# Two layers of cross attention and experts: Silu written through tanh, and part of the convolution and of the last residuals moved from VectorE to ScalarE and GpSimd

## The chip, the cores and the metric

The kernel runs on one core of a Trainium2 chip. The metric is device time in microseconds (us), the median of several runs. The engines of the core are named as in the profile: PE (TensorE, matrix products) with PEld (its weight load), DVE (VectorE), ACT (ScalarE), POOL (GpSimd) and SP (SyncE, which issues transfers). Each engine works through its own queue of instructions in order and waits for the others by semaphores.

## The reference, cut to what matters

`x` has 2 sequences of 1024 tokens with 256 features. Two layers of attention and experts follow each other, each added to `x`:

```python
x = x + L0_xattn(ctx, layernorm(x))    # 16 heads of 64; 77 context rows ask, 1101 keys
x = x + L0_ffn(layernorm(x))           # 8 experts, the best 2 of each token, Relu inside;
                                       # its own last step is a layernorm with gamma, beta
x = x + L1_xattn(layernorm(x), ctx)    # 16 heads of 16, 77 keys, causal
x = x + L1_ffn(layernorm(x))

# L1_ffn, with h its input and cw the weights of the best 2 of 8 experts
g, u = h @ Wg[e], h @ Wu[e]                        # e = 0..3
routed = sum(cw[e] * ((silu(g) * u) @ Wd[e]))
routed += (cw[4] + cw[6]) * h + cw[7] * relu(h)    # experts without a matrix
shared = causal convolution of h over 4 tokens, feature by feature, + conv_b
return routed + shared
```

All is float32. The two places that the change touches are `silu(g) * u` and the convolution of the last step, and the layernorm that ends `L0_ffn` for tokens of the last quarter: `x + (a - mean) * rstd * gamma + beta`, where `a` is the layer's input plus what the experts gave.

## The kernel before, in words

The tokens lie in 16 tiles of 128 rows (`xr[:, t, :]`), four tiles to a block, so that the last quarter is block 3 with tiles 12 to 15. The first layer's attention takes the greater part of the run. Then come 39 slots, each one expert's work on 128 gathered tokens (`up`, `down`, lines 1230 to 1265). Beside the later slots, and after the last one, the second layer runs, block by block, in numbered steps `k`; this part begins around 1400 us, and the last slot ends near 1540 us.

The order of the instructions on every engine is written out by hand: `tc.manual_schedule` (line 1666) keeps all five queues in the order in which the program calls its functions. There is no planner that moves anything. Four tables say what is called in a step: `pre` and `mid` (attention: `project`, `turn_back`, `divide`, `attend`), `rest` (the second expert layer's `up` and `down`) and `fill` (all else). A step first does its attention part with `score`, `turn_step` and `soften` (softmax: maximum and subtraction on DVE, lines 1322 and 1323, Exp on ACT, line 1324), then `rest`, then `fill` (lines 1715 to 1721).

What the change touches:

- `Mix.up(e)` (line 1503) multiplies the block's 512 tokens by `Wg[e]` and `Wu[e]` (line 1510, tile `pg`), applies Silu on ACT (line 1518, tile `sl`, 128 x 512) and multiplies by the second product on DVE (line 1522, tile `hid`). `Mix.down(e)` multiplies `hid` by `Wd[e]` (line 1533) and adds the weighted result to `xr` on DVE (line 1541). There are 16 pairs, four to a block. Those of blocks 0 to 2 come in steps 18 to 43, beside attention; those of block 3 come last, in steps 45 to 52, with no attention left.
- `Mix.convolve(c)` (line 1481) is called twice a block, in the steps of `up(1)` and `up(2)`: the first term on ACT (line 1487) and three taps on DVE (line 1491), all of them into the one tile `cv`. `Mix.convolved` turns it back and adds it to `xr` (lines 1500 and 1501). `Mix.copies` (lines 1475 to 1479) treats the experts without a matrix, with two ACT operations and two POOL additions of 128 x 256 for each tile; it is called in steps next to those of `convolve`.
- `way(t, put)` (line 1585) lays out the path of tile `t` from the first expert layer to the second attention, in successive steps: `weigh` (line 1018) and `measure(0, t)`, then `residual(t)` (lines 1032 and 1033, two DVE operations) and `measure(1, t)` (statistics of the new `xr`, line 141 ff. on DVE, the power -0.5 on POOL, line 156), then `shift(1, t)` (line 1027) and `normal(t)` (line 1040 on ACT, line 1041 on POOL), then the transposes and the queries. For tiles 12 to 15 this goes in `fill`, a step apart, between steps 22 and 29; for the tiles before, it goes beside the slots. `gather(t)` (line 1001, two indirect transfers issued by POOL) precedes it.

POOL's queue in this part holds gathers, the powers of the statistics, line 1041 and the additions of `copies`.

Of the kernel before, what the change touches and what calls it, by code (L numbers as in the profile page):

```python
# [8 lines left out]
F32 = mybir.dt.float32  # L9
I32 = mybir.dt.int32  # L10
AF = mybir.ActivationFunctionType
ALU = mybir.AluOpType
# [4 lines left out]
P = 128  # L17
# [3 lines left out]
NBLK = 4  # L21
# [25 lines left out]
E1, EM, I1, KC = 8, 4, 128, 4  # L47
# [3 lines left out]
def tile_two_layers(ctx: ExitStack, tc: tile.TileContext, a: dict, out: bass.AP):  # L51
    nc = tc.nc
# [12 lines left out]
    xr = const.tile([P, NT, D], F32, tag="xr", name="xr")  # L65
# [423 lines left out]
    side = {}  # L489
# [75 lines left out]
    with ExitStack() as st:  # L565
# [5 lines left out]
        ps_s = st.enter_context(tc.tile_pool(name="a_ps_s", bufs=1, space=PSUM))  # L571
# [50 lines left out]
        def contexts():  # L622
            src = [ctx_sb[:, b, :] for b in range(B)]
            stats = ln_stats(src)
            ch = lnp.tile([C, B, D], F32, tag="ch", name="ch")
            yield
            ln_apply([ch[:, b, :] for b in range(B)], src, stats)
            for b in range(B):
                for c in range(2):
                    pt = ps_t.tile([P, 512], F32, tag="t", name="pt")  # L630
                    nc.tensor.transpose(pt[:, :C], ch[:, b, c * P : (c + 1) * P], ident[:C, :C])
                    nc.vector.tensor_scalar(
                        kvT[b][:, c, S:NKEY], pt[:, :C], ln1w[:, c : c + 1], ln1b[:, c : c + 1], ALU.mult, ALU.add
                    )
# [202 lines left out]
        with tc.manual_schedule(engines=ORDERED):  # L837
# [14 lines left out]
            c = contexts()  # L852
# [31 lines left out]
            for n in range(2):  # L884
                m, s, v, t = latents(2 + n)
# [102 lines left out]
    got, stat, qT_of, h_at, hT_at = {}, {}, {}, {}, {}  # L988
# [24 lines left out]
    def acc(t):  # L1013
        return tok[t // 8][:, t % 8, :]
# [15 lines left out]
    def residual(t):  # L1030
        mv, rstd = stat.pop((0, t))
        nc.vector.scalar_tensor_tensor(acc(t), acc(t), mv[:, 0, 0:1], gamma, ALU.subtract, ALU.mult)
        nc.vector.scalar_tensor_tensor(xr[:, t, :], acc(t), rstd[:, :1], xr[:, t, :], ALU.mult, ALU.add)


    def normal(t):

        nb, rstd = stat.pop((1, t))
        h = h_at[t] = en.tile([P, D], F32, tag="h", name="h")
        nc.scalar.activation(h, xr[:, t, :], AF.Identity, bias=nb[:, :1], scale=rstd[:, :1])  # L1040
        nc.gpsimd.tensor_tensor(xr[:, t, :], xr[:, t, :], bo1, ALU.add)
# [48 lines left out]
    en = ctx.enter_context(tc.tile_pool(name="en", bufs=2, side="right", reuse_waits="tile"))  # L1090
    ps_h = ctx.enter_context(tc.tile_pool(name="b_ps_h", bufs=2, space=PSUM, reuse_waits="tile"))
    ps_o = ctx.enter_context(tc.tile_pool(name="b_ps_o", bufs=1, space=PSUM, reuse_waits="tile"))
    extra, first, spare = ExitStack(), ExitStack(), ExitStack()

    ps_x = spare.enter_context(tc.tile_pool(name="b_ps_x", bufs=1, space=PSUM, reuse_waits="tile"))
    hp = ctx.enter_context(tc.tile_pool(name="b_h", bufs=2, side="right", reuse_waits="tile"))
    yp = ctx.enter_context(tc.tile_pool(name="b_y", bufs=2, side="right", reuse_waits="tile"))
    xp = ctx.enter_context(tc.tile_pool(name="b_x", bufs=3, side="right", reuse_waits="tile"))
    xe = first.enter_context(tc.tile_pool(name="b_xe", bufs=1, side="right", reuse_waits="tile"))

    fw = [
# [1 line left out]
        for i in range(4)  # L1103
    ]
    xs_of = {s: xe.tile([P, D], F32, tag=f"xs{s}", name="xs") for s in (*range(3, NA), 2, 0, 1)}
    at_p = ps_s = None
    later = {}

    def table():
# [65 lines left out]
    def ask_rows(s):  # L1175

        r0 = entry(nc.sync, s, 1)
        xs = xs_of[s] if s < NA else xp.tile([P, D], F32, tag="xs", name="xs")
        nc.sync.dma_start(out=xs, in_=tab_x[bass.ds(r0, TB), :])
        rows_of[s] = xs  # L1180
# [37 lines left out]
    def turn_rows(s):  # L1218
        xs = rows_of.pop(s)
        pt = ps_t.tile([P, 512], F32, tag="t", name="px")  # L1220
        for c in range(2):
            nc.tensor.transpose(pt[:, c * TB : (c + 1) * TB], xs[:, c * P : (c + 1) * P], ident)
        xT = xp.tile([P, 2, TB], F32, tag="xT", name="xT", bufs=2)
        evac(xT.rearrange("p c q -> p (c q)"), pt[:, : 2 * TB], to=nc.vector)
        return xT

    def hidden(s):
        return hp.tile([P, NF, TB], F32, tag="hT", name="hT")
# [163 lines left out]
    class Mix:  # L1392
# [88 lines left out]
        def convolve(self, c):  # L1481

            if c == 0:
                self.cv = at_p.tile([P, 2, 512], F32, tag="cv", name="cv", bufs=1)
            cv = self.cv[:, c, :]
            src = hT2[self.b][:, c, self.off - KC + 1 : self.off + 512]
            nc.scalar.activation(
                cv, src[:, :512], AF.Identity, bias=cb1[:, c : c + 1], scale=cw1[:, c * KC : c * KC + 1]
            )
            for k in range(1, KC):  # L1490
                nc.vector.scalar_tensor_tensor(
                    cv, src[:, k : k + 512], cw1[:, c * KC + k : c * KC + k + 1], cv, ALU.mult, ALU.add
                )
# [9 lines left out]
        def up(self, e):  # L1503
            ps = []
            for w in (wg1, wu1):
                ups[0] += 1
                pool = ps_x if ps_x is not None and ups[0] % 3 == 0 else ps_h
                ps.append(pool.tile([P, 512], F32, tag="h", name="pg"))
                for c in range(2):
                    nc.tensor.matmul(  # L1510
                        ps[-1],
                        w[:, e, c, :],
                        hT2[self.b][:, c, self.off : self.off + 512],
                        start=(c == 0),
                        stop=(c == 1),
                    )
            sl = rp.tile([P, 2, 512], F32, tag="tT", name="sl", bufs=1)[:, 0, :]
            nc.scalar.activation(sl, ps[0], AF.Silu)

            hid = const.tile([P, 2, D], F32, tag="l1w" + "kv"[e % 2], name="hid").rearrange("p c d -> p (c d)")  # L1520
            self.hid[e] = hid
            nc.vector.tensor_tensor(hid, sl, ps[1], ALU.mult)

        def down(self, e):
            hid = self.hid.pop(e)
# [59 lines left out]
    def way(t, put):  # L1585

        put(1, weigh, t)
        put(1, measure, 0, t)
        put(2, residual, t)
        put(2, measure, 1, t)  # L1590
        put(3, shift, 1, t)
        put(3, normal, t)
        put(4, turned, t)
        put(5, queries, t)
# [13 lines left out]
    def put(where, k, f, *args):  # L1608
        where.setdefault(k, []).append((f, args))
# [18 lines left out]
    for t in range(12, NT):  # L1628
        k = K1 + t - 12
# [7 lines left out]
    for n, (blk, e) in enumerate(halves):  # L1637
        m = mix[blk]
        k = at_step[2 * n : 2 * n + 2]
# [12 lines left out]
    def run_all(where, k):  # L1652
        for f, args in where.pop(k, []):
            f(*args)
# [11 lines left out]
    with tc.manual_schedule(engines=ORDERED | {mybir.EngineType.SP}):  # L1666
        ask_rows(0)
        ask(0)
        ask_rows(1)
        ask(1)  # L1670
        for s in range(2, NA):
            if s < 4:
                ask(s)
            ask_rows(s)
        xT = turn_rows(0)
        r3.measure()
        r3.stats()
        prev, k = None, 0
        for s in range(NSLOT):
            hT = hidden(s)  # L1680
            up(s, xT, hT, 0)
            for f in todo.pop(s, []):
                f()
            if s > S1:
                step(k)
                run_all(fill, k)
            up(s, xT, hT, 1)
            if s + 1 < NSLOT:
                xT = turn_rows(s + 1)
            if s == NA:  # L1690
                first.close()
            if prev is not None:
                down(*prev)
                ask_later(s)
            if s == S1:
                extra.close()
                spare.close()
                ps_x = None
                kbd, v1p, causal = spread["s"]
                at_p = ctx.enter_context(tc.tile_pool(name="c_at", bufs=1, reuse_waits="tile"))  # L1700
                ps_s = spare.enter_context(tc.tile_pool(name="c_ps_s", bufs=1, space=PSUM, reuse_waits="tile"))
                step(k)
                run_all(fill, k)
            if s >= S1:
                step(k + 1)
                run_all(rest, k)
                run_all(rest, k + 1)
                run_all(fill, k + 1)
                k += 2
            prev = s, hT  # L1710
            for f in todo.pop(s + 0.5, []):
                f()
        down(*prev)
        assert not todo and k == K1, todo
        for k in range(K1, K3 + 8):
            if k == K3:
                spare.close()
                ps_x = ctx.enter_context(tc.tile_pool(name="d_ps_x", bufs=1, space=PSUM, reuse_waits="tile"))
            step(k)
            run_all(rest, k)  # L1720
            run_all(fill, k)
        mix[-1].down(EM - 1)
        assert not fill and not pre and not mid and not rest, (fill, pre, mid, rest)
# [59 lines left out]
```

## Time and profile before

| | us |
|---|---|
| median of 3 runs | 1721.43 (1720.8 to 1727.57) |
| the profiled execution | 1722.1 |
| its span | 1720.4 |
| PE busy in the span | 1634.9 (95%) |
| DVE | 1077.2 (63%) |
| POOL | 850.1 (49%) |
| ACT | 732.7 (43%) |
| mean granted PE clock | 0.988 of full speed |

The shares are means over unlike stages: POOL's 850 us are nearly all from the first attention, and after 1530 us POOL is busy for some 44 of 190 us. A matrix product's end is modelled in the trace, so a busy PE need not be PE at its peak. In the chain of waits, each line is the piece of work, or the wait for none that the profile shows ("issue"), that the end of the run is followed back through.

### The profile page before, as it was taken

Reading aid. Unit: us, or ns where it says so; the run is one execution under the profiler, and the core shown is the slowest. Engines: PE = TensorE matmul, PEld = TensorE weight load, DVE = VectorE, ACT = ScalarE, POOL = GpSimd, SP = SyncE. Lnnn points to the kernel's source line nnn. Section 1 sums busy time; section 2 is a strip of 40 time slices with the busy share of each in tenths; the row PEclk is TensorE's granted clock in tenths of the full one; section 3 lists DMA queues with packets and bytes.
Section 4 is the critical chain, followed back from the end, with each engine's and each line's share of the span. In section 5 each row is a group of like instructions: output and inputs, shape, how many; then the busy total and the mean of one; then the engine's idle time right before and its main releaser. Section 6 shows DMA issues by size and latency. Waiting matters only on the chain.

```text
span 1720.4 us, 25127 instructions
## 1 busy us (share of the span) xinstructions
PE 1634.9 (95%) x9348; PEld 1047.2 (61%) x9348; DVE 1077.2 (63%) x2149; ACT 732.7 (43%) x1423; POOL 850.1 (49%) x538
## 2 busy tenths in 40 slices
PE   6998999999999999999999999899999999998798
PEld 3544555555555555565555555458898978875555
DVE  5766766666666667677767776655322376547666
ACT  1544445444444444444444444531221245555743
POOL 1277657765775677566875686604040233013211
PEclk9999999999999999999999999999999999998999
DMA  3011211212112210000000000048879967510000
GB/s 118 25 50 61 74 68 68 74 68 80 64 69 77 74 59 4 19 7 1 13 13 7 13 13 28 1 145 290 295 263 319 355 221 226 160 40 19 13 13 25
DMA packets 124863, 151.94 MB, mean 88 GB/s; under 512 B 13212, under 2 KB 112710, under 8 KB 124742
## 3 DMA queue, kind: packets, MB, share of 16 engines
q1 hardware_dynamic: 79984, 102.18, 18.0%
q10 hardware_dynamic: 41685, 39.77, 6.6%
q0 software_dynamic: 3072, 8.39, 1.4%
q8 instruction: 74, 1.21, 0.3%
q14 instruction: 48, 0.39, 0.1%
HBM read 105.10 MB, written 45.22 MB: 87 GB/s over the span
## 4 chain that ended last, share of the span: by engine, by line
PE 70%; DVE 14%; ACT 7%; POOL 5%; issue 2%; DMA 2%; SPq 0%; ACTq 0%; DVEq 0%
PE sc L746 13%; PE ptr L798 12%; PE po L823 8%; PE pqk L676 7%; PE ph L1238 7%; PE po L1257 6%; POOL pa L780 5%; DVE nm L756 5%; ACT pa L757 4%; PE pv L652 3%; PE py L691 3%; PE pg L1510 2%; PE ptr L1334 1%; PE sb L721 1%; ACT pT L118 1%
## 5 line engine op out<-in xcount | busy, mean ns | idle before, releaser
L780 POOL TENSOR_SCALAR pa<-pa,f 128x1024 f32<-128x1024 f32 x244 | 694.8, 2865 | 364.4 <-ACT pT L118 258.1
L757 ACT ACTIVATE pa<-sc,nm 128x1024 f32<-128x1024 f32 x256 | 282.9, 1109 | 427.5 <-DVE nm L756 424.4
L756 DVE TENSOR_REDUCE nm<-sc 128x1 f32<-128x1024 f32 x256 | 301.3, 1218 | 138.1 <-PE sc L746 138.1
L798 PE MATMUL ptr<-ident,pa 128*128 128x128 f32 x2048 | 285.5, 278 | 27.0 <-DVE kT L122 6.2
L798 PEld LDWEIGHTS ptr<-ident,pa 128*128 128x128 f32 x2048 | 225.1, 141 | 110.2 <-issue 61.9
L823 PE MATMUL po<-pT,v 128*64 128x512 f32 (+1 forms) x1152 | 262.6, 598 | 0.0
L746 PE MATMUL sc<-kT,qT 64*128 64x512 f32 x1024 | 258.8, 624 | 0.0
L122 DVE COPY pT<-ptr 128x512 f32<-128x512 f32 x256 | 175.6, 688 | 100.5 <-PE ptr L798 97.3
L118 ACT COPY pT<-ptr 128x512 f32<-128x512 f32 (+1 forms) x320 | 177.4, 586 | 134.9 <-PE ptr L798 131.5
L823 PEld LDWEIGHTS po<-pT,v 128*64 128x64 f32 (+1 forms) x1152 | 78.5, 136 | 153.8 <-issue 148.7
L1238 PE MATMUL ph<-xT,w 128*128 128x128 f32 x1248 | 148.5, 276 | 2.4 <-DVE xT L122 0.9
L1238 PEld LDWEIGHTS ph<-xT,w 128*128 128x128 f32 x1248 | 144.7, 192 | 4.6 <-issue 2.5
L1257 PE MATMUL po<-w,hT 128*128 128x256 f32 x624 | 141.2, 379 | 0.5 <-issue 0.5
L746 PEld LDWEIGHTS sc<-kT,qT 64*128 64x128 f32 x1024 | 89.8, 189 | 84.8 <-issue 81.0
L1257 PEld LDWEIGHTS po<-w,hT 128*128 128x128 f32 x624 | 115.6, 190 | 16.4 <-issue 2.3
L1251 DVE TENSOR_SCALAR hT<-ph,bs 128x128 f32<-128x128 f32 x156 | 44.0, 344 | 104.1 <-PE ph L1238 95.7
L156 POOL TENSOR_TENSOR rstd<-ve,neghalf 128x1 f32<-128x1 f32 (+2 forms) x45 | 32.2, 716 | 142.8 <-DVE ve L149 123.8
L1249 ACT ACTIVATE hT<-ph,bs 128x128 f32<-128x128 f32 x156 | 44.4, 367 | 119.9 <-PE ph L1238 97.9
L1001 POOL DMA_INDIRECT yt<-tab_y,pos x32 | 32.0, 1000 | 94.4 <-PE po L1257 82.2
L676 PE MATMUL pqk<-kvT,wk 128*128 128x512 f32 (+1 forms) x192 | 72.3, 506 | 0.0
L652 PE MATMUL pv<-wv,kvT 128*128 128x256 f32 (+1 forms) x288 | 69.2, 382 | 2.9 <-DVE pB L732 2.3
L652 PEld LDWEIGHTS pv<-wv,kvT 128*128 128x128 f32 (+1 forms) x288 | 52.3, 185 | 25.1 <-issue 16.2
(253 smaller groups left out, 1837.4 us busy)
## 6 DMA issues: line engine op xcount, KB each, us to landing
w<-in_L_ffn_W_dram SPq DMA_DIRECT2D x78, 1024.0 KB
tab_x<-zero ACTq DMA_DIRECT2D x32, 512.0 KB
tab_y<-zero ACTq DMA_DIRECT2D x32, 512.0 KB
xs<-tab_x SPq DMA_DIRECT2D x39, 128.0 KB
tab_y<-y ACTq DMA_DIRECT2D x39, 128.0 KB
xr<-in_x_dram SPq DMA_DIRECT2D x4, 512.0 KB
wq<-in_L_xattn_Wq_dram SPq DMA_DIRECT2D x8, 256.0 KB
wk<-in_L_xattn_Wkv_dram SPq DMA_DIRECT2D x8, 256.0 KB
```

What stands on the lines that cost most here:

```text
L118: nc.scalar.copy(dst, src)
L122: nc.vector.tensor_copy(dst, src)
L652: nc.tensor.matmul(ps[:r, n * GC : (n + 1) * GC], kvT[b][:, c, kt * P : kt * P + r], groups[G]["v"][:, c, :], start=(c == 0), stop=(c == 1),)
L676: nc.tensor.matmul(ps[:, : n1 - n0], groups[G][nm][:, c, p * P : (p + 1) * P], kvT[b][:, c, n0:n1], start=(c == 0), stop=(c == 1),)
L746: nc.tensor.matmul(sc[j][:, n * 512 : (n + 1) * 512], U.qT[j * DH0 : (j + 1) * DH0, q0 : q0 + P], U.kT[j * DH0 : (j + 1) * DH0, n * 512 : ...
L756: nc.vector.tensor_reduce(U.nm[:, 0, r : r + 1], sc[j], AX.X, ALU.max, negate=True)
L757: nc.scalar.activation(U.pa[t][:, j, :], sc[j], AF.Exp, bias=U.nm[:, 0, r : r + 1], accum_out=U.l[:, 0, r : r + 1])
L780: nc.gpsimd.tensor_scalar_mul(pa, pa, f)
L798: nc.tensor.transpose(ps[:, n * P : (n + 1) * P], U.pa[t][:, j, kt * P : (kt + 1) * P], ident)
L823: nc.tensor.matmul(U.po[j * DH0 : (j + 1) * DH0, :], v[:r, kt, h0 : h0 + DH0], U.pT[j][:r, kt, :], start=(kt == 0), stop=(kt == NKT - 1),)
L1238: nc.tensor.matmul(ps[:, n * TB : (n + 1) * TB], w1[:, c, f * P : (f + 1) * P], xT[:, c, :], start=(c == 0), stop=(c == 1),)
L1257: nc.tensor.matmul(ps[:, :D], hT[:, f, :], w2[:, f, :], start=(f == 0), stop=(f == NF - 1))
```

## The change

Three edits, all in the second layer's part. `d_mp` is a new pool of two tiles of 128 x 512 for the taps; it is opened after the last slot, when three pools of the slots are closed for it.

```diff
+    def residual_aside(t):
+
+        nb, rstd = stat.pop((0, t))
+        nc.scalar.activation(acc(t), acc(t), AF.Identity, bias=nb[:, :1], scale=rstd[:, :1])
+        nc.gpsimd.tensor_tensor(acc(t), acc(t), gamma, ALU.mult)
+        nc.gpsimd.tensor_tensor(xr[:, t, :], xr[:, t, :], acc(t), ALU.add)
...
@@ convolve
-            for k in range(1, KC):
+            for k in range(1, KC - 1):
+                tap = mp.tile([P, 512], F32, tag="tap", name="tap")
+                nc.scalar.activation(
+                    tap, src[:, k : k + 512], AF.Copy, scale=cw1[:, c * KC + k : c * KC + k + 1]
+                )
+                nc.gpsimd.tensor_tensor(cv, cv, tap, ALU.add)
+            for k in range(KC - 1, KC):
                 nc.vector.scalar_tensor_tensor(
                     cv, src[:, k : k + 512], cw1[:, c * KC + k : c * KC + k + 1], cv, ALU.mult, ALU.add
                 )
...
@@ up
-            nc.scalar.activation(sl, ps[0], AF.Silu)
+            if self.blk == NBLK - 1:
+                nc.scalar.activation(sl, ps[0], AF.Silu)
+            else:
+
+                nc.scalar.activation(sl, ps[0], AF.Tanh, scale=0.5)
+                nc.vector.scalar_tensor_tensor(sl, sl, 1.0, ps[0], ALU.add, ALU.mult)
...
-            nc.vector.tensor_tensor(hid, sl, ps[1], ALU.mult)
+            if self.blk == NBLK - 1:
+                nc.vector.tensor_tensor(hid, sl, ps[1], ALU.mult)
+            else:
+                nc.vector.scalar_tensor_tensor(hid, sl, 0.5, ps[1], ALU.mult, ALU.mult)
...
@@ way
-        put(2, residual, t)
+        if t < 12:
+            put(2, residual, t)
+        else:
+            put(2, shift, 0, t)
+            put(2, residual_aside, t)
         put(2, measure, 1, t)
...
@@ after the last slot
+        slots.close()
+        mp = ctx.enter_context(tc.tile_pool(name="d_mp", bufs=2, reuse_waits="tile"))
```

Silu of `g` is `g * (1 + tanh(g / 2)) / 2`. For blocks 0 to 2, ACT computes the tanh, one new DVE operation adds 1 and multiplies by `g`, and the factor 0.5 goes into the multiplication by `u`, which stays one DVE operation. Block 3 keeps Silu. In the convolution, taps 1 and 2 become a scaled copy on ACT and an addition on POOL each; tap 3 stays on DVE, last, in the same tile. For tiles 12 to 15 the normalized residual is computed by one small DVE operation (`shift(0, t)`), one ACT operation and two POOL operations in place of two DVE operations. The pools `hp`, `yp` and `xp` of the slots are entered on a stack of their own so that they can be closed.

More of the change, by code (lines that the diff above doesn't have):

```diff
@@ L1092, in tile_two_layers @@
     ps_o = ctx.enter_context(tc.tile_pool(name="b_ps_o", bufs=1, space=PSUM, reuse_waits="tile"))
-    extra, first, spare = ExitStack(), ExitStack(), ExitStack()
+    slots, extra, first, spare = ExitStack(), ExitStack(), ExitStack(), ExitStack()
     ps_x = spare.enter_context(tc.tile_pool(name="b_ps_x", bufs=1, space=PSUM, reuse_waits="tile"))
-    hp = ctx.enter_context(tc.tile_pool(name="b_h", bufs=2, side="right", reuse_waits="tile"))
-    yp = ctx.enter_context(tc.tile_pool(name="b_y", bufs=2, side="right", reuse_waits="tile"))
-    xp = ctx.enter_context(tc.tile_pool(name="b_x", bufs=3, side="right", reuse_waits="tile"))
+    hp = slots.enter_context(tc.tile_pool(name="b_h", bufs=2, side="right", reuse_waits="tile"))
+    yp = slots.enter_context(tc.tile_pool(name="b_y", bufs=2, side="right", reuse_waits="tile"))
+    xp = slots.enter_context(tc.tile_pool(name="b_x", bufs=3, side="right", reuse_waits="tile"))
     xe = first.enter_context(tc.tile_pool(name="b_xe", bufs=1, side="right", reuse_waits="tile"))
@@ L1105, in tile_two_layers @@
     xs_of = {s: xe.tile([P, D], F32, tag=f"xs{s}", name="xs") for s in (*range(3, NA), 2, 0, 1)}
-    at_p = ps_s = None
+    at_p = ps_s = mp = None
     later = {}
```

## The prediction

> **What bounds the kernel now.** I read first the page for the span and busy shares, then busy time by stretch of 20 us over the last part of the run (everything the change touches lies after 1530 us), then the chain of waits there in order of time, and last the instruction groups for prices. The stretches, from the windows view (columns: TensorE, its weight load, VectorE, ScalarE, GpSimd busy, granted clock, DMA share, GB/s):
>
> ```profile
> span 1720.4 us, 25127 instructions
> ...
> 1550.00:1570.00 20.00, 14.94 (x77) 9.44 (x75) 16.04 (x38) 14.26 (x24) 9.34 (x10) 0.83 0.10 28
> 1590.00:1610.00 20.00, 16.07 (x90) 11.13 (x89) 13.04 (x33) 14.31 (x29) 6.97 (x10) 1.00 0.08 27
> 1610.00:1630.00 20.00, 14.86 (x87) 9.41 (x85) 14.09 (x30) 15.36 (x26) 3.93 (x7) 0.92 0.01 1
> ```
>
> No engine is full: TensorE idles 4 to 5 us in each, ScalarE and VectorE have 4 to 7 us to spare. So the stage is bound by handovers between in-order queues, and what counts is when a result is there, not how much work an engine has. The chain shows which:
>
> ```profile
> 1608.38 0.72 ACT cv L1487
> 1609.10 0.03 issue
> 1609.13 0.76 DVE cv L1491
> 1609.89 0.03 issue
> 1609.92 0.76 DVE cv L1491
> 1610.68 0.03 issue
> 1610.70 0.75 DVE cv L1491
> 1611.45 0.33 DVE xr L1387
> 1611.79 0.72 DVE mx L1322
> 1612.51 0.02 issue
> 1612.53 0.81 DVE pr L1323
> 1613.34 0.04 issue
> 1613.38 0.79 PE sc L1301 x4
> ```
>
> The reader is to see that the convolution's taps on VectorE are on the path: the softmax of the next attention step queues behind them, and TensorE waits for that. All eight convolutions stand so in the chain (start of the taps: 1547.17, 1563.94, 1609.13, 1625.06, 1664.48, 1672.51, 1702.03 just beside it, 1707.19). From 1578.4 to 1600.0 the chain is VectorE almost without a break: router, normalized residuals, statistics.
>
> **Prices**, from the groups of the last 320 us, shapes apart:
>
> ```profile
> L1518 ACT ACT_TABLE_LOAD x10 | 12.8, 1283 | 2.1 <-PE pg L1510 2.0
> L1475 ACT ACTIVATE y<-h,cw 128x256 f32<-128x256 f32 x16 | 7.9, 496 | 1.6 <-DVE cw L1466 1.6
> L1476 POOL TENSOR_TENSOR xr<-xr,y 128x256 f32<-128x256 f32 x16 | 11.7, 728 | 110.5 <-ACT y L1475 96.4 <-DVE xr L1541 14.0
> ```
>
> **Part 1, Silu by tanh (12 of 16).** Now ScalarE changes its function table 19 times after 1530 us (10 before Silu, 6 before softmax's Exp, 3 before the router's Exp), 19 x 1.283 = 24.4 us. If Tanh and Exp share a table, 18 go (only the last quarter's one change to Silu stays): 23.1 us of ScalarE. Against it stand 12 new VectorE operations of 128x512; the nearest row is a convolution tap, 0.75 us: 9 us. The Trainium skill weighs heavier here: "ScalarE: Activation LUTs", What ACT_TABLE_LOAD costs, adds a drain of about 1.38 us to each change, 2.66 us, so 48 us. The trace has no such drain: the load of 1542.51 starts 0.02 us after the copy before it and Exp follows at 1543.81. I take 1.283. (That the set with exp also holds tanh is stated in its Table sets section; no row here shows it.)
>
> Most of this is off the path. At 1533.41, 1549.56, 1565.99, 1573.21, 1575.12, 1590.12, 1595.37, 1604.55, 1610.97, 1625.99, 1637.38, 1639.29 and 1685.34 ScalarE had to wait for TensorE or VectorE after the load anyway, or VectorE was not ready for the product; that wait hides the load, and without it each would be worth its 1.28 us. Five loads are on the chain: 1542.51, 1544.54, 1558.19, 1619.53, 1653.53. The new VectorE step lies before `hid`; where `hid` waits for the second product (L1510) it costs nothing, and where VectorE itself is the chain (1593.65) it costs 0.75.
>
> **Part 2, convolution (8 times).** VectorE loses two of three taps (16 x 0.755 = 12.1 us), ScalarE gains 16 copies with a scale (0.496 for 256 columns plus 256 more at 0.83 ns, the step between that row and the 0.80 of L1487 less its extra bias: 0.71 us each, 11.4 us), GpSimd gains 16 adds of 128x512. No row has that add. From below: the Trainium skill ("GPSIMD Engine Reference", 3.1) gives 4.497 us for 2048 columns; with our 0.728 for 256 that is 2.10 ns a column, an estimate of 1.27 us. From above: twice 0.728, 1.46. I take 1.36, twice the row less one fixed part of about 0.1 (a one-column memset on GpSimd takes 0.095).
>
> But the last tap works in place on what GpSimd leaves, so three taps in a row on one engine become a relay. Before: first term (0.80) and three taps (2.33) end 3.2 us after the convolution's start. After: first term, first copy ready at 1.42, first add 1.5 to 2.9, second add to 4.3, last tap to 5.1. VectorE holds in order behind the last tap: statistics and evacuations, then the next softmax, for which TensorE waits. Each is 1.9 us later if VectorE came at once and GpSimd is free. Place by place (change of the time at which VectorE comes free, loads of part 1 included):
> - First, 1546.3: two loads gone from ahead of it, it starts 2.2 us earlier: -0.3.
> - Second, 1563.1: 0.8 earlier by a load less, a new step more; but in GpSimd's queue two gathers (L1001, about 1.0 each and 0.3 between) stand ahead of the adds until 1565.6. Adds to 1568.4, tap to 1569.15 instead of 1566.27: +2.9, the first place contained.
> - Third, 1608.3: GpSimd free, +1.9. Fourth, 1624.2: a load less, a new step more (-0.5): +1.4.
> - The load of 1653.53 is on the chain: -1.25.
> - Fifth and sixth, 1662.6 and 1670.6: VectorE came 1.2 us late before, +0.9; the sixth's adds stand behind four GpSimd adds of `copies`, themselves behind the late VectorE: +1.75 for both.
> - Seventh, 1700.1: +0.85, swallowed by the wait for TensorE at 1706.6. Eighth, 1705.3: four `copies` adds are ahead until 1709.55, adds to 1712.35, tap to 1713.15 instead of 1710.36: +2.8. Behind it only VectorE's last 6.7 us remain, so it moves the end.
>
> Convolutions and loads: 2.9 + 1.9 + 1.4 - 1.25 + 1.75 + 2.8 = +9.5 us.
>
> **Part 3, residual of tiles 12 to 15.** Now two VectorE operations, and the statistics directly behind them (timeline):
>
> ```profile
> 1580.24 0.15 DVE L1027 SCALAR_TENSOR_TENSOR nb<-mv,rstd 128x1 f32<-128x1 f32 x1
> 1580.31 0.48 DVE L1032 SCALAR_TENSOR_TENSOR tok<-tok,mv,gamma 128x256 f32<-128x256 f32 x1
> ...
> 1580.89 0.48 DVE L1033 SCALAR_TENSOR_TENSOR xr<-tok,rstd,xr 128x256 f32<-128x256 f32 x1
> 1581.10 0.86 POOL L1041 TENSOR_TENSOR xr<-xr,bo 128x256 f32<-128x256 f32 x1 [4.43 <-ACT h L1040]
> 1581.41 0.43 DVE L141 BATCH_NORM_STATS2 st<-xr 128x6 f32<-128x256 f32 x1
> ```
>
> After: one small VectorE operation (0.15), a ScalarE pass like L1040 (0.60) queued behind the L1040 of the tile before, two GpSimd operations of 0.73 behind L1041. For tile 13: ScalarE to 1581.55, GpSimd L1041 to 1581.9, gamma to 1582.65, sum to 1583.4, statistics at 1583.5 instead of 1581.41: +2.1, although VectorE has 0.8 us less work. Behind the statistics wait the next tile's weighing, the router's second half, `hid`, the softmax. Tiles 13 to 15 lie in the VectorE chain: +6.3. Tile 12 (1570) is 1.6 late, inside VectorE's idle 2.17 us at 1576: nothing; without that cover, 1.6. The new step before `hid` at 1593.65: +0.75.
>
> **Sum:** 9.5 + 6.3 + 0.75 = +16.5 us. Longer pauses of TensorE have a second price: after 1.14 us of work in 1624 to 1628 the granted clock was 0.50 from 1628 to 1636, about 4 us lost. One more such stretch may come or not; I take +1 (0 to 5). Contention I leave at nothing: the eighth's three taps took 3.17 instead of 2.33 beside GpSimd adds, but VectorE now mostly waits while GpSimd adds. The profiled run is 1722.1 us with a span of 1720.4; the median of the runs, 1721.43, is 0.7 below it. 1721.43 + 17.5 = **1738.9 us**. With adds at 1.27 or 1.46 it moves by 1.5 either way, and with VectorE waiting 1.6 or 2.6 per residual by another 1.5; with the clock, 1732 to 1745 is this case's own range.
>
> **Rivals.**
> - *Faster: cover.* If VectorE reaches the last tap later than the relay ends, each convolution saves its 1.5 us (12), each residual 0.8 (3.2), the chain's loads 3.8 less 2.3 of new steps: -16.7, 1705 us. It decides at each place: gain begins when VectorE comes more than about 2 us after the first term ends. The profile shows 0.1 us (first, third) to 1.2 us (fifth to eighth), so against; for it, VectorE has slack that an earlier ScalarE could reshuffle. 0.12.
> - *Waits half covered:* the relays (9.5 + 6.3, and about 3 that the loads' gain hides in them: 18.8) bite in half of the places: 9.4 - 3 + 0.75, about +7, less what a cheaper add leaves off: 1727 us, no change that can be told. 0.12.
> - *Cold clock:* pauses beyond 3 us at 1569, 1582, 1592 bring two more stretches at 0.50: +17 + 8, 1746 us. 0.12.
> - *The change does not do what it says:* Tanh brings its own table, loads stay. The loads' gains (about 2 at the first two places, 0.5, 1.25) are gone: +21, 1742 us. 0.06.
> - Forecast: 0.58.
>
> **Numbers.** The kernel's measurement tells about 0.5% (8.6 us) from no change. Slower: 0.58 + 0.12 + 0.06 = 0.76; within 0.5%: 0.12; faster: 0.12. The range 1724 to 1752 takes in the half-covered case and the cold clock and leaves out the faster one and the far end.
>
> **What would show it.** Right: one table load left after 1560; VectorE idle 2 to 4 us ahead of each last tap, put down to GpSimd; about 1.3 to 1.4 us per add; statistics after the residual waiting for GpSimd some 2 us three times; ScalarE busy about 9 us less, which buys nothing. Wrong: taps that find GpSimd done, adds well under 1.2 us, or TensorE's pauses shrinking at 1564 and 1621 because ScalarE delivers earlier.

## The result, and the profile after

The changed kernel takes 1740.63 us (median of 6 runs, 1736.52 to 1744.0), the kernel before 1721.7 us (6 runs, 1720.0 to 1727.57). The ratio is 1.0104, with a 95% interval of 1.0083 to 1.0124: 18.9 us between the medians, 17.9 by the ratio, 1.0% slower. The profiled execution of it, the fastest of the six, took 1736.52 us with a span of 1734.8. Its mean granted clock was 0.988, as in the profiled execution of the kernel before; in the other five it was 0.982 to 0.984.

The page and the windows view of the changed kernel, the same stretches as before (its own times; columns: TensorE, its weight load, VectorE, ScalarE, GpSimd, granted clock, DMA share, GB/s):

```profile
span 1734.8 us, 25138 instructions
...
1550.00:1570.00 20.00, 13.11 (x70) 8.05 (x66) 12.41 (x30) 10.08 (x20) 10.97 (x12) 0.91 0.10 28
1590.00:1610.00 20.00, 15.07 (x61) 9.39 (x61) 11.90 (x43) 7.21 (x18) 7.41 (x11) 0.83 0.08 27
1610.00:1630.00 20.00, 17.80 (x92) 11.34 (x91) 10.94 (x24) 12.58 (x26) 8.02 (x11) 0.91 0.00 1
```

VectorE and ScalarE are less busy in each of these stretches (VectorE 35.3 us in the three together, against 43.2), and the kernel is slower. Over the whole run ScalarE lost 11.9 us of work and VectorE 8.6, and GpSimd gained 25.7. The chain of waits at the third convolution shows where the time is:

```profile
1615.95 0.71 ACT cv L1494
1616.66 0.62 ACT tap L1499
1617.28 0.07 issue
1617.35 1.28 POOL cv L1502
1618.63 0.07 issue
1618.70 1.28 POOL cv L1502
1619.97 0.03 issue
1620.00 0.75 DVE cv L1504
1620.75 0.33 DVE xr L1394
1621.08 0.72 DVE mx L1329
1621.80 0.02 issue
1621.82 0.81 DVE pr L1330
```

The three taps on one engine have become the relay ScalarE, GpSimd, GpSimd, VectorE. From the first term's start to the next maximum it is 5.1 us now and was 3.4. The waits of VectorE, the longest first (us in total, times, the longest):

```profile
DVE cv L1504 <- POOL cv L1502: 24.5, 7, 5.8
DVE sl L1536 <- ACT sl L1535: 23.1, 10, 6.0
DVE st L141 <- POOL xr L1040: 11.1, 4, 3.0
DVE cv L1504 <- POOL hT L1427: 6.1, 1, 6.1
```

The first and the last are the convolution's last tap behind GpSimd, in eight places of eight (for one of them the profile names the clearing of `hT` that stands beside the addition in GpSimd's queue). In the kernel before, the first tap waited for ScalarE's first term alone. The third is the statistics behind the new residual. The second is the new step behind ScalarE's tanh; it stands where `hid` waited before:

```profile
DVE hid L1522 <- ACT sl L1518: 19.3, 5, 7.2
DVE hid L1522 <- PE pg L1510: 12.1, 6, 3.8
...
DVE cv L1491 <- ACT cv L1487: 5.3, 3, 2.8
```

The prices of the new operations, from the groups with shapes apart:

```profile
L1502 POOL TENSOR_TENSOR cv<-cv,tap 128x512 f32<-128x512 f32 x16 | 20.3, 1268 | 16.2 <-ACT tap L1499 15.6
...
L1499 ACT ACTIVATE tap<-hT,cw 128x512 f32<-128x512 f32 x16 | 10.6, 711 | 0.0
L1536 DVE SCALAR_TENSOR_TENSOR sl<-sl,pg 128x512 f32<-128x512 f32 x12 | 8.2, 686 | 23.1 <-ACT sl L1535 23.1
...
L1532 ACT ACT_TABLE_LOAD x1 | 1.3, 1283 | 0.0
```

One table load of nineteen is left, so Tanh and Exp do share a table. And the residual of tile 13 in the timeline:

```profile
1581.43 0.22 DVE L1027 SCALAR_TENSOR_TENSOR nb<-mv,rstd 128x1 f32<-128x1 f32 x2
1581.62 0.60 ACT L1047 ACTIVATE h<-xr,nb,rstd 128x256 f32<-128x256 f32 x1 [2.05 <-DVE nb L1027]
1582.13 0.58 ACT L1038 ACTIVATE tok<-tok,nb,rstd 128x256 f32<-128x256 f32 x1
1582.30 0.72 POOL L1048 TENSOR_TENSOR xr<-xr,bo 128x256 f32<-128x256 f32 x1 [2.67 <-ACT h L1047]
1582.98 0.72 POOL L1039 TENSOR_TENSOR tok<-tok,gamma 128x256 f32<-128x256 f32 x1
1583.78 0.72 POOL L1040 TENSOR_TENSOR xr<-xr,tok 128x256 f32<-128x256 f32 x1
1584.54 0.43 DVE L141 BATCH_NORM_STATS2 st<-xr 128x6 f32<-128x256 f32 x1 [2.88 <-POOL xr L1040]
```

From the small operation to the statistics it is 3.1 us, where it was 1.2; VectorE stands still for 2.88 of them.

**A measure for the stage.** The part ahead of the second experts is the same in all kernels here, but its length varies: the first product of the second experts (L1510 before) started at 1525.0 to 1537.6 us in the profiles of this study; why is not shown. So beside the times I give the *stage*: from that start to the end of the span. Before: 1720.4 - 1531.95 = 188.45 us. After: 1734.8 - 1530.65 = 204.15, that is +15.7. The stage varies between executions, too: three kernels below were profiled twice, and their two stages differ by 1.9, 2.7 and 3.2 us, the longer one each time with more time at a granted clock of 0.50 (by 5.8, 9.6 and 6.3 us). So a stage tells no differences below about 3 us by itself. Between the starts of the 16 products of `up`, the stage grew so (us, after less before):

| stretch, and what stands in it | growth |
|---|---|
| to the 3rd product (first convolution) | -0.5 |
| to the 4th (second convolution) | +3.0 |
| to the 5th and 6th (residuals of tiles 13 to 15; tile 12 stands at the boundary before) | +1.9, +4.45 |
| to the 7th and 8th (third and fourth convolution) | +2.9, +0.5 |
| to the 9th and 10th | +0.1, 0.0 |
| to the 11th to 13th (fifth and sixth convolution) | +0.7, 0.0, +0.55 |
| to the 14th to 16th (seventh) | -0.2, 0, 0 |
| to the end (eighth) | +2.4 |

### The profile page after: what moved, and what is told of

It reads as the page before. It is cut to its first block, busy times and chain, and to the rows that moved or that the text cites. A ratio compares the mean times of both kernels' runs of the same rounds, so it can differ in the third digit from the quotient of the medians.

```text
span 1734.8 us, 25138 instructions
## 1 busy us (share of the span) xinstructions
PE 1637.1 (94%) x9348; PEld 1047.8 (60%) x9348; DVE 1068.6 (62%) x2141; ACT 720.8 (42%) x1425; POOL 875.8 (50%) x562
## 4 chain that ended last, share of the span: by engine, by line
PE 69%; DVE 12%; ACT 7%; POOL 6%; DMA 3%; issue 2%; ACTq 0%; SPq 0%; POOLq 0%; DVEq 0%
PE sc L746 13%; PE ptr L798 12%; PE po L823 8%; PE pqk L676 7%; PE ph L1245 7%; PE po L1264 6%; DVE nm L756 5%; POOL pa L780 5%; ACT pa L757 4%; PE pv L652 3%; PE py L691 3%; PE pg L1523 2%; PE ptr L1341 1%; PE sb L721 1%; ACT pT L118 1%
## 5 line engine op out<-in xcount | busy, mean ns | idle before, releaser
L676 PE MATMUL pqk<-kvT,wq 128*128 128x512 f32 x128 | 64.8, 629 | 3.0 <-DMA wq<-in_L_xattn_Wq_dram 3.0
```

Source lines behind the costliest of these rows:

```text
L676: nc.tensor.matmul(ps[:, : n1 - n0], groups[G][nm][:, c, p * P : (p + 1) * P], kvT[b][:, c, n0:n1], start=(c == 0), stop=(c == 1),)
```

## The experiments

My theory was that in-order handovers set the time: a result that GpSimd brings late stops VectorE's queue, whatever the engines' work. The rival was that the work counts: either VectorE's and ScalarE's relief pays where waits are covered, or GpSimd's added work and its sharing with VectorE cost by themselves. Each ratio is to the kernel before, run beside the kernel on the same chip; times in us are the ratio times that kernel's median.

### Each part alone

The tanh alone:

```diff
-            nc.scalar.activation(sl, ps[0], AF.Silu)
+            if self.blk == NBLK - 1:
+                nc.scalar.activation(sl, ps[0], AF.Silu)
+            else:
+                nc.scalar.activation(sl, ps[0], AF.Tanh, scale=0.5)
+                nc.vector.scalar_tensor_tensor(sl, sl, 1.0, ps[0], ALU.add, ALU.mult)
...
+                nc.vector.scalar_tensor_tensor(hid, sl, 0.5, ps[1], ALU.mult, ALU.mult)
```

> The kernel before with the tanh alone; convolution and residuals stay on VectorE. Handover theory (mine): 18 table loads go from the trace, 23 us of ScalarE, but only the few on the chain count, each less a new VectorE step of 0.69: about -1.6 at the first two convolutions, -0.5 at the fourth, -1.25 at the load of 1653.53, +0.7 at 1593.65, so -2.7 us against the kernel before, in -1 to -5. Rival (ScalarE is what TensorE's pauses wait for): the relief closes the pauses at 1564 and 1621 and the cold clock behind them, -8 us or more.

Measured: 1716.09 us, ratio 0.9986 (0.9977 to 0.9996), -2.4 us; stage 187.57, -0.9. Some 23 us of table loads went and about a tenth of that shows. The rival's -8 is out.

The convolution's relay alone is the changed kernel with Silu and the residual put back:

```diff
-            for k in range(1, KC):
+            for k in range(1, KC - 1):
+                tap = mp.tile([P, 512], F32, tag="tap", name="tap")
+                nc.scalar.activation(tap, src[:, k : k + 512], AF.Copy, scale=cw1[:, c * KC + k : c * KC + k + 1])
+                nc.gpsimd.tensor_tensor(cv, cv, tap, ALU.add)
+            for k in range(KC - 1, KC):
```

> The kernel before with the convolution's middle taps by ScalarE and GpSimd alone; Silu and the residuals as before. Handover theory: each relay ends 1.7 us later than three taps did where GpSimd is free, 3 to 4 where gathers or the additions of copies stand ahead, 0.7 where VectorE came late: 1.7 + 3.4 + 1.7 + 1.7 + 0.7 + 0.9 + 2.6, about +12.7 us against the kernel before (+9 to +16). Rival (cover): VectorE has 12 us less work and comes late enough, -5 us or less.

Measured: 1734.61 us, ratio 1.0086 (1.0068 to 1.0104), +14.8 us; stage 201.99, +13.5. VectorE waited 25.3 us in seven places for GpSimd before the last tap.

The residual of the last quarter alone:

```diff
-        put(2, residual, t)
+        if t < 12:
+            put(2, residual, t)
+        else:
+            put(2, shift, 0, t)
+            put(2, residual_aside, t)
```

> The kernel before with the residual of tiles 12 to 15 on ScalarE and GpSimd alone. Handover theory: the statistics start 2.1 us later for tiles 13 to 15, nothing for tile 12, +6.3 us against the kernel before (+4 to +9). Rival (cover): 3.2 us less VectorE work in a stretch where VectorE is the chain, -3 us.

Measured: 1724.6 us, ratio 1.0029 (1.0019 to 1.0039), +5.0 us; stage 194.58, +6.1. The statistics waited 11.0 us for GpSimd in four places. The three parts add to -2.4 + 14.8 + 5.0 = +17.4, and together they gave +17.9 (1.0104): a cost that only the three together have cannot be told within these intervals (3 to 7 us wide). In the stage the parts add to 18.7 against 15.7, in traces with unlike clocks: the relay alone had 0.50 for 39.0 us of its stage, the changed kernel for 32.2.

### The same work in another order

```diff
+            for k in range(KC - 1, KC):
+                nc.vector.scalar_tensor_tensor(cv, src[:, k : k + 512], cw1[:, c * KC + k : c * KC + k + 1], cv, ALU.mult, ALU.add)
             for k in range(1, KC - 1):
                 tap = mp.tile([P, 512], F32, tag="tap", name="tap")
                 nc.scalar.activation(tap, src[:, k : k + 512], AF.Copy, scale=cw1[:, c * KC + k : c * KC + k + 1])
                 nc.gpsimd.tensor_tensor(cv, cv, tap, ALU.add)
-            for k in range(KC - 1, KC):
-                nc.vector.scalar_tensor_tensor(cv, src[:, k : k + 512], cw1[:, c * KC + k : c * KC + k + 1], cv, ALU.mult, ALU.add)
```

> The changed kernel with one thing exchanged: the one tap that stays on VectorE comes directly after ScalarE's first term, and the two GpSimd additions after it. The same instructions on the same engines[...]; only VectorE no longer waits for GpSimd. Handover theory: VectorE is free 1.6 us after the convolution starts, not 4.9 (and not 3.2 as in the kernel before), in seven places; of the 18.9 us lost, about 20 come back, and the kernel stands at -6 to +5 us against the one before, the residual's +6.3 still in it. Rival (it is the amount of GpSimd work, or its sharing with VectorE, that costs): the time stays within 4 us of the changed kernel's, +15 to +20.

Measured: 1716.8 us, ratio 0.9981 (0.9973 to 0.9989), -3.3 us; stage 185.43, -3.0. This is the run that decides. The instructions are those of the changed kernel; exchanging the order of the two loops took 1.0104 to 0.9981. The timeline at its third convolution:

```profile
1607.45 0.83 ACT L1494 ACTIVATE cv<-hT,cb,cw 128x512 f32<-128x512 f32 x1
1608.16 1.34 ACT L1503 ACTIVATE tap<-hT,cw 128x512 f32<-128x512 f32 x2
1608.32 0.75 DVE L1498 SCALAR_TENSOR_TENSOR cv<-hT,cw,cv 128x512 f32<-128x512 f32 x1 [1.84 <-ACT cv L1494]
...
1609.24 2.63 POOL L1506 TENSOR_TENSOR cv<-cv,tap 128x512 f32<-128x512 f32 x2 [5.24 <-DVE cv L1498]
1609.32 0.79 DVE L1329 TENSOR_REDUCE mx<-sc 128x8 f32<-128x616 f32 x1
```

The maximum of the next softmax starts 1.9 us after the first term, beside the two additions and not behind them. So neither GpSimd's 20 us of additions nor their running beside VectorE is what cost the time. The stage agrees place by place: from product to product this kernel and the changed one grow alike where the residuals stand (+1.9 and +4.4 us in both), and the 18.7 us between them come where the convolutions stand (3.2 us up to the 4th product, 10.5 from the 6th to the 9th, 2.8 from the 10th to the 13th, 2.4 at the end).

A part of it comes by way of the clock. Between the 7th and the 9th product, the granted clock was 0.50 for 10.2 us in the kernel before and in the changed kernel, and full in this trace; in the whole stage it was 0.50 for 32.2 us in the changed kernel and 29.4 here. Over all executions its mean was 0.983 in the changed kernel and 0.986 here, which is an estimate of 5 us of full speed in 1720. Even if all of that were lost time, some 16 of the 21 us would be the order's own; whether TensorE's longer pauses are what brings the lower clock is not shown here.

With the residual back on VectorE (the line `put(2, residual, t)` for all tiles):

> The changed kernel with the VectorE tap first, as in the run before it, and with the residual of tiles 12 to 15 back on VectorE. Handover theory: the residual's relay cost 4.6 us alone, so this stands about 4.6 below the run with the tap first: -8 us against the kernel before (-5 to -11), and below the tanh alone, too, by about 4. Rival (with the tap first other waits hide the residual's): as the run with the tap first, -3.

Measured: 1718.8 us beside 1723.9, ratio 0.9972 (0.9964 to 0.998), -4.8 us; stage 184.97, -3.5. The sign is right and the size is not: 1.5 us below the run before, where 4.6 were expected. Up to the sixth product of `up` the profile with the residual's relay loses 4.8 us against this one, as expected, but nearly all of it is made up later: this one then has a granted clock of 0.50 to 0.65 from 1626 to 1634 us, where the other stays at full speed. In the other executions the clock does not explain it: its mean is 0.986 in both kernels. So where the rest of the 4.6 us stays is open, and the rival, that other waits hide a part of the residual's, is not excluded.

### Two steps that went otherwise

Copies and additions a step later, so that they do not stand ahead of ScalarE's evacuations:

```diff
+        def convolve_rest(self, c):
             ...
             for k in range(1, KC - 1):
                 tap = mp.tile([P, 512], F32, tag="tap", name="tap")
...
             put(fill, k[0], m.convolve, e - 1)
+            put(fill, k[0] + 1, m.convolve_rest, e - 1)
```

> As the run before it, and the two scaled copies with their GpSimd additions are issued at the end of the next step, so that they no longer stand ahead of ScalarE's evacuations in the convolution's own step (at the fourth convolution 1.2 us of copies lay on the chain ahead of an evacuation that TensorE waited for). Handover theory: 1 to 3 us less than the run before it. Rival (these 1.4 us are hidden, or come back a step later): within 1 us of it.

Measured: 1722.57 us beside 1723.9, ratio 0.9993 (0.998 to 1.0005), -1.2 us; stage 183.15, -5.3. The time contradicted the expectation and the stage did not, so I ran both kernels again, together with the tanh alone:

> The kernel with tanh and the VectorE tap first, residual on VectorE, once more beside the next two on one chip. Handover theory: in the stage from the first product of the second experts to the end 3.5 us less than the kernel before, as in its first profile; whole time -3 to -8.

> The kernel with the copies and additions a step later, once more. Its first profile had the stage 5.3 us shorter than in the kernel before, but 4.7 us more ahead of the stage, where nothing differs and weights are loaded. If that part is chance of the run, its whole time now stands 1 to 2 us below the run listed before it; if the step later costs by itself, it stands 2 us or more above again, and the stage shows it.

> The tanh alone once more, on the chip of the other two. Handover theory: -1 to -4 us against the kernel before; 2 to 4 us above the kernel with the tap first. Rival (the tap's new place is worth nothing): within 1 us of it.

Measured, beside 1719.9 us: the tap first 1714.42, ratio 0.9974 (0.9964 to 0.9984), -4.5 us, stage 182.25; a step later 1719.29, ratio 1.0002 (0.999 to 1.0014), +0.3 us, stage 186.34; the tanh alone 1718.82, ratio 0.9993 (0.9984 to 1.0003), -1.2 us, stage 185.69. So the step later costs by itself, 3.6 and 4.8 us in the two comparisons, against the expectation of a gain. The second trace of it shows one place:

```profile
1572.74 2.61 POOL L1510 TENSOR_TENSOR cv<-cv,tap 128x512 f32<-128x512 f32 x2
1575.41 0.50 PEld L1517 LDWEIGHTS pc<-ident,cv 128*128 128x128 f32 x3 [3.61 <-POOL cv L1510]
1575.41 0.90 PE L1517 MATMUL pc<-ident,cv 128*128 128x128 f32 x3 [3.06 <-POOL cv L1510]
```

The additions, now behind the next step's gathers in GpSimd's queue, end after TensorE has come to transpose `cv`: TensorE waits 3.06 us. By the fifth product of `up` this kernel is 2.1 us behind the other in the first pair of traces and 4.0 in the second. In the second it ends 4.1 us behind, as the times have it; in the first it makes the loss up and ends 1.8 ahead in the stage. The clock tells these pairs apart: it was 0.50 for 26.3 and 26.8 us of the stage in the second pair, but for 35.9 us in the tap first and 20.5 in the step later in the first. So the second pair is the one that compares like with like, and the first trace of the step later was lucky. The tanh alone is a gain of 1.2 to 2.4 us, in one of two comparisons not told from none; the tap first was 3.3 us below it on the chip where both ran.

### The residual's work without its wait

The kernel before, with the change's four operations beside the residual, into a tile that nobody reads:

```diff
+    def beside(t):
+        mv, rstd = stat[0, t]
+        nb = small.tile([P, 4], F32, tag="nb", name="nb")
+        nc.vector.scalar_tensor_tensor(nb[:, :1], mv[:, :1, 0], -1.0, rstd[:, :1], ALU.mult, ALU.mult)
+        s = mp.tile([P, D], F32, tag="spare", name="spare")
+        nc.scalar.activation(s, acc(t), AF.Identity, bias=nb[:, :1], scale=rstd[:, :1])
+        nc.gpsimd.tensor_tensor(s, s, gamma, ALU.mult)
+        nc.gpsimd.tensor_tensor(s, s, gamma, ALU.add)
...
+        if t >= 12:
+            put(2, beside, t)
         put(2, residual, t)
```

> The kernel before, with the residual of tiles 12 to 15 computed on VectorE as before, and beside it the change's small VectorE operation, ScalarE pass and two GpSimd operations of the same size into a tile that nobody reads. The work of the residual's relay without its wait, and with more VectorE work than either kernel. Handover theory: 0 to +1.5 us against the kernel before (the small operation 4 x 0.15, the ScalarE pass 0.6 ahead of one evacuation). Rival (it is ScalarE's and GpSimd's work, or memory sharing with VectorE, that made the residual alone cost 4.6 us): +4 us or more.

Measured: 1728.68 us beside 1723.9, ratio 1.0033 (1.002 to 1.0045), +5.7 us; stage 192.75, +4.3: the rival's number. But the trace shows that the edit had brought in a wait of its own. `residual` overwrites the tile that ScalarE's pass reads:

```profile
1575.79 0.61 ACT L1040 ACTIVATE spare<-tok,nb,rstd 128x256 f32<-128x256 f32 x1
1576.43 0.48 DVE L1032 SCALAR_TENSOR_TENSOR tok<-tok,mv,gamma 128x256 f32<-128x256 f32 x1 [0.75 <-ACT spare L1040]
1576.49 1.02 POOL L1041 TENSOR_TENSOR spare<-spare,gamma 128x256 f32<-128x256 f32 x1 [3.78 <-ACT spare L1040]
1576.95 0.83 DVE L1033 SCALAR_TENSOR_TENSOR xr<-tok,rstd,xr 128x256 f32<-128x256 f32 x1
```

VectorE waits for ScalarE four times, 4.1 us in all. So the pass was given a constant tile to read:

```diff
-        nc.scalar.activation(s, acc(t), AF.Identity, bias=nb[:, :1], scale=rstd[:, :1])
+        nc.scalar.activation(s, zero, AF.Identity, bias=nb[:, :1], scale=rstd[:, :1])
```

> As the residual beside, but ScalarE's pass reads a constant tile. In the run before, VectorE's own residual wrote over what that pass read, so VectorE waited 4.1 us for ScalarE in four places: a new wait that the edit brought in by itself. Now the same four operations run beside the residual and nobody waits for them. Handover theory: what is left is the small VectorE operation (0.15) and the sharing with GpSimd (the residual's second operation took 0.83 instead of 0.485, the first 0.56 instead of 0.477) at three places on the chain, about 0.6 each: +0.5 to +2.5 us against the kernel before, in the stage from the first product of the second experts to the end. Rival (the amount of work on ScalarE and GpSimd costs): +4 us or more there.

Measured: 1721.16 us beside 1719.9, ratio 1.0003 (0.9995 to 1.0011), +0.5 us; stage 188.96, +0.5. In its trace VectorE waits for none of the new operations, and the statistics follow its own residual at once. What is left is that GpSimd's two operations now run beside VectorE's weighing of the next tile (L1018) and stretch it; first the kernel before, then this run:

```profile
1582.16 0.99 DVE L1018 SCALAR_TENSOR_TENSOR tok<-yt,wts,tok 128x256 f32<-128x256 f32 x2
...
1580.89 0.48 DVE L1033 SCALAR_TENSOR_TENSOR xr<-tok,rstd,xr 128x256 f32<-128x256 f32 x1
...
1581.41 0.43 DVE L141 BATCH_NORM_STATS2 st<-xr 128x6 f32<-128x256 f32 x1
...
1581.92 0.72 POOL L1041 TENSOR_TENSOR spare<-spare,gamma 128x256 f32<-128x256 f32 x1
...
1582.16 1.63 DVE L1018 SCALAR_TENSOR_TENSOR tok<-yt,wts,tok 128x256 f32<-128x256 f32 x2
```

That is 0.64 us, and twice 0.64 is what the stage grows by to the 5th and 6th product; with 0.3 before, the residuals' stretch is 1.6 us longer than in the kernel before, against 6.15 in the residual alone, and 1.0 of it comes back by the ninth product. The whole time shows none of it that can be told from chance, at the same mean granted clock over all executions (0.9875 in both kernels). So most of the residual's 5 us is its wait; running beside VectorE has a price, but a small one.

## Why the prediction was right

It gave 1738.9 us, in a range of 1724 to 1752; measured were 1740.63. By its steps:

- **Handovers, not work, bind the stage.** Right, and shown twice: by the exchange of order (21 us between two orders of the same instructions, at most about 5 of them by the clock) and by the residual's work beside (+0.5 us, with 1.6 in its own stretch).
- **Table loads mostly off the path.** Right: 18 of 19 went, and the tanh alone gave -2.4 and -1.2 us. The drain that the Trainium skill ("ScalarE: Activation LUTs", What ACT_TABLE_LOAD costs) adds did not show in the profile before, and a gain of 1 to 2 us gives no sign of it. The one term of this part that failed is the load of 1653.53, put at -1.25: it left out the new VectorE step (0.69), which the forecast counts at other places. `hid` came 0.6 us earlier there, and the next product of `up` not at all (stretch to the 10th: 0.0). The load stood on the chain, but in its place stand now the new step and `hid`, ahead of an evacuation that TensorE needs (two lines of the chain before, then the chain after):

```profile
1653.53 1.28 ACT L1518
...
1655.88 0.66 PE ptr L1334 x4
...
1665.03 0.70 DVE sl L1536
...
1665.83 0.69 DVE hid L1543
1666.52 0.34 DVE xr L1394
...
1666.90 0.66 PE ptr L1341 x4
```

  The transposes start 5.2 us after the ninth product of `up` in both kernels.
- **The relay of the convolution.** Right in kind at all eight places. The addition took 1.268 us: the estimate from the Trainium skill's figure and our row ("GPSIMD Engine Reference", 3.1: 1.27) was exact, and my 1.36, twice the row less a fixed part, too high. Place by place, forecast against growth of the stage: first and second +2.9, measured +2.5; third and fourth +3.3, measured +3.4; fifth and sixth +1.75, measured +1.25; eighth +2.8, measured +2.4. GpSimd's queue in front of the additions was what made the second and the eighth long, as worked out; towards its end, the chain of the changed kernel has four additions of `copies`, then the convolution's. VectorE's waits were 2.2 to 6.1 us, longer in four places than the 2 to 4 named: at the third and fourth VectorE came before the first term had begun, at the second and eighth GpSimd's queue was in front.
- **The residual.** 6.3 + 0.75 forecast for tiles 13 to 15 with the new step before `hid`, 1.9 + 4.45 = 6.35 measured in the stage; alone 5.0 in time and 6.1 in the stage. Each wait was 2.8 us (11.1 over four), where some 2 were forecast; tile 12, put at nothing, cost 0.3 in the residual alone.
- **The clock.** This term was too small. Over its six executions the changed kernel had a mean granted clock of 0.983, the kernel before 0.987 to 0.988 on the three chips of the experiments (the relay alone 0.983, too): an estimate of 7 us of full speed lost, where 1 (0 to 5) was allowed. Not all of that need be lost time. In the two profiled executions the clocks are nearer: 0.50 for 28.9 us of the stage before and for 32.2 after, 1.6 us of full speed.
- **The sum.** 16.5 us forecast in the stage, 15.7 in the profiled execution. That execution was the fastest of six and had the highest clock; the other five took 1.2 to 7.5 us more, at 0.982 to 0.984, and the median difference is 18.9. So the mechanism is right, but that the total fits to 2 us is in part luck: the handovers were put 0.8 us too high and the clock too low.

Of the rivals, the covered relay needs VectorE to come late; it waited in all eight places, which answers the half-covered case, too. Tanh brought no table of its own. The cold clock was in part true: not in the profiled execution, but in the other five.

## What to carry to other kernels

Where engines pass results along in fixed order and none is full, moving work to an idle engine pays only if nobody in a busy queue stands right behind the result. Before moving an operation, look at the next reader in its queue and at what already stands ahead in the receiving queue; put the part that stays first, and let the moved part end while its reader is still far off. A control experiment has readers and writers of its own, too: look in its trace for waits that it brings, before believing its number.

The version that beats both kernels keeps tanh, puts VectorE's tap first and leaves the residual on VectorE: 0.9972 and 0.9974 of the kernel before, in two comparisons.

## What the runs showed of the hardware that I had not expected

- GpSimd and VectorE slow each other in some pairs: in the residual beside, VectorE's second operation took 0.83 us against 0.485 alone and GpSimd's multiplication 0.90 to 1.02 against 0.72, when both ran at once. With the constant tile these two did not meet and were at their usual length, but GpSimd's operations met VectorE's next ones (L1018), which took 0.76 and 0.83 us instead of 0.475 and 0.485. In the changed kernel VectorE mostly waited while GpSimd added, and no addition took more than 1.277 us.
- A GpSimd addition of two inputs took 0.728 us for 256 columns and 1.268 for 512: 2.1 ns a column and about 0.19 us besides.
- In all traces the granted clock was either full or 0.50, and the stretches at 0.50 lasted 3.4 us or two, three or four times that. One such stretch more or less is 1.7 us of full speed, so two executions of one kernel can differ by some us in their stage.
